# Half of the softmax transposes moved from TensorE to VectorE and DMA in a four-layer conditioned transformer

## The chip, the cores and the metric

The kernel runs on one core of a Trainium2 chip, in one launch. The metric is the device time in microseconds, the median of the runs shown. All data are 32-bit floats.

## The reference

Eight sequences of 256 tokens with 512 features pass through four layers, each steered by a conditioning vector per sequence.

- Layer 0: RMS norm, attention with 8 query heads of width 64 and one key and value head, rotary embedding; then a gated MLP of width 2048 (SiLU).
- Layer 1: layer norm with scale and shift, attention with 16 heads of width 32 on normalised queries and keys, an added bias, a gated residual; then an MLP of width 2048 (GELU).
- Layer 2: layer norm, attention with 16 query heads and 4 key and value heads of width 32, rotary embedding, and a block-sparse mask.
- Layer 3: eight small two-layer experts over slices of 64 features, a layer norm, SiLU and an output product.

What the change touches is the middle of each attention. For one head it is

```
s = q @ k.T (+ bias or mask)          # 256 x 256
p = exp(s - max(s))                   # rows are queries
y = (p @ v) / sum(p)
```

`p @ v` is summed over the keys. TensorE sums over the partitions, so p, which comes with queries on the partitions, has to be turned so that keys lie there.

## The kernel before, in words

**Scheduling.** The program is written against a layer that places tiles in buffers, sets the semaphores, and plans the order in which each engine's queue gets its instructions: it simulates the program and issues what is ready in the simulation, older instructions first. So an instruction can be issued ahead of an older one of the same engine. On the chip each queue then runs in that order. All DMAs of the kernel are issued from SP's queue (SyncE).

**Attention.** `attend` runs all three attentions. It works on groups of four heads: 2 groups per sequence in layer 0, 4 in layers 1 and 2, so 16, 32 and 32 groups. One iteration of its loop does, in the order of the source:

1. `scored`: the scores of the next group, for four heads and two query tiles, into four PSUM banks of tag `A` (line L645). Heads lie on separate groups of rows of the array and run side by side.
2. `turned` for heads 0 and 1 of the group before: each 128x128 block of p is transposed by TensorE with the identity (L702) into a bank of tag `C`, and `copy` brings it back over p, head 0 by VectorE (L460), head 1 by ScalarE (L464). A head has four blocks, and three in layer 2, where a tile of keys is hidden.
3. `softmax` of the next group: per head and query tile the row maximum (L659 in layer 0; L667, fused with the bias or mask, in layers 1 and 2) on VectorE, then the exponential with its row sum on ScalarE (L672). Then the reciprocals of the sums are turned, written to DRAM (`spread`, L685) and read back as a broadcast (L690).
4. `some`: a stretch of queued work. Generators hold the projections of the next sequence, the output product of the last one and sums of weights; each `some(quantum)` runs a share of it. `rest` runs all that is left, at the start of each sequence.
5. `turned` for heads 2 and 3 of the group before, then `some` again.
6. `weighted`: p @ v for the group before (L717), into one bank of tag `C`, and `divided`: the product with the broadcast reciprocals (L732, VectorE) into `ctxT`. A last `some`.

At the end of the layers 0 and 1 the last group's weighted sum is placed beside the start of the MLP (`then`, `mlp_begin`).

**Buffers.** p has 7 buffers of 128x512, one head each. `ctxT` has 6 of 128x256. `qk` has 4 of 128x512.

**Turning by blocks.** The normalised inputs of most sequences are already turned without TensorE: `prepare` writes them in an interleaved order, VectorE transposes every 32x32 block of the tile in one instruction (L515, 128x1024), four DMAs write it to DRAM (`turn`, L520), and `fetch` reads it back with the blocks in their places (L533 in one DMA, L539 in eight).

**MLP.** `mlp` of the layers 0 and 1 multiplies 2x2 blocks with seven products in place of eight (L908 up, L955 down). `blocked` and `blocked_again` hold the right-hand sums in three tiles of `ctxT` (for the first sequence in `qk`). L908 reads its moving operand from the turned tiles in runs of 32 elements. `sums` takes one p buffer per product. The tail of each MLP runs the next layer's first projection as queued work.

Of the kernel before, what the change touches and what calls it, by code (L numbers as in the profile page):

```python
# [25 lines left out]
F32 = mybir.dt.float32  # L27
# [6 lines left out]
P = 128  # L34
# [7 lines left out]
    "n": 4, "hT": 2, "qT": 2, "kT": 2, "v": 2, "ctxT": 6, "p": 7, "qk": 4, "row": 3, "wbig": 8,  # L42
# [48 lines left out]

def constants():
# [15 lines left out]
        "mask2": np.ascontiguousarray(mask),  # L108
    }


def layout(inputs):
# [10 lines left out]
    def grouped(w):  # L123
# [20 lines left out]
        "bias": np.ascontiguousarray(a["mask_1x1xSxS_ff0"].reshape(S, S)),  # L144
        "vec": np.ascontiguousarray(np.concatenate([vec[k] for k in VEC], 1)),
# [26 lines left out]
class Program:  # L172
# [50 lines left out]
    def setup(self):  # L223
# [40 lines left out]
        self.n_turn = 0  # L264
        self.half_pi = c([P, 1], "half_pi")
# [190 lines left out]
    def copy(self, i, out, in_, scale=None):  # L456

        if i % 2 == 0:
            if scale is None:
                self.nc.vector.tensor_copy(out, in_)  # L460
            else:
                self.nc.vector.tensor_scalar(out, in_, scale, None, ALU.mult)
        elif scale is None:
            self.nc.scalar.copy(out, in_)  # L464
        else:
            self.nc.scalar.activation(out, in_, AF.Copy, scale=scale)

    def modulated(self, i, out, in_, scale, shift):
        if shift is None:
            self.copy(i, out, in_, scale)  # L470
        elif i % 2 == 0:
            self.nc.vector.tensor_scalar(out, in_, scale, shift, ALU.mult, ALU.add)
        else:
            self.nc.scalar.activation(out, in_, AF.Identity, bias=shift, scale=scale)
# [27 lines left out]
    def prepare(self, name, b, quick=False):  # L502
# [14 lines left out]
        self.n_turn += 1  # L517
        to = kept.rearrange("(c i) (a x) -> a i c x", c=4, a=4)
        for a in range(4):
            nc.sync.dma_start(  # L520
                to[a], hT[32 * a : 32 * a + 32, :].rearrange("p (c x) -> p c x", c=4)
            )
        self.ready[name, b] = [hT, None, kept, 0]
# [17 lines left out]
    def h(self, name, b, quick=False):  # L541
# [16 lines left out]
        def placed(i, c, in_):  # L558
            scale = mod[:, scale_at + c, b : b + 1]
            shift = None if shift_at is None else mod[:, shift_at + c, b : b + 1]  # L560
            self.modulated(i, place[:, c], in_, scale, shift)

        if rows is None:
            for c in range(KC):
                placed(c, c, place[:, c])
# [43 lines left out]
    def attend(self, name, n_groups, hd, project, value, finish, work, key_tiles=(2, 2), biased=None,  # L609
# [27 lines left out]
        def scored(b, g):  # L637
# [3 lines left out]
            for j0 in range(0, 4, rows):  # L641
                for q in range(TB):
                    for j in range(j0, j0 + rows):
                        lhsT, rhs = lhs_rhs[j]
                        nc.tensor.matmul(  # L645
                            s[j][:, at[q] : at[q] + wide[q]], lhsT(q), rhs(wide[q]),
# [4 lines left out]
        def softmax(s):  # L651
            tot = self.t([P, 4, TB], "tot", 3)
            lows = self.t([P, 4, TB], "low", 3)
            ps = []
            for j in range(4):
                p = self.bank("p")[:, :total]
# [5 lines left out]
                for q in range(TB):  # L662
                    cols = slice(at[q], at[q] + wide[q])
                    src, sign = s[j], 1.0
                    if biased is not None:

                        nc.vector.tensor_tensor_reduce(  # L667
                            p[:, cols], s[j][:, cols], biased[:, cols], -1.0, BIG, ALU.add,
                            ALU.min, low[:, q : q + 1],
                        )  # L670
                        src, sign = p, -1.0
                    nc.scalar.activation(  # L672
                        p[:, cols], src[:, cols], AF.Exp, bias=low[:, q : q + 1], scale=sign,
                        accum_out=tot[:, j, q : q + 1],
                    )
                ps.append(p)
# [18 lines left out]
            return ps, by  # L695

        def turned(j, p):
# [9 lines left out]
            self.copy(j, p, m[:, :total])  # L707

        def weighted(b, g, pT):
            o = self.bank("C")  # L710
            for c in range(nch):
                for k in range(TB):
                    mine = [n for n, (kk, q) in enumerate(pairs) if kk == k]
                    q0 = pairs[mine[0]][1]
                    for i in range(per):
                        j = c * per + i
                        nc.tensor.matmul(  # L717
                            o[i * hd : (i + 1) * hd, c * S + q0 * P : (c + 1) * S],
                            value(got[b][1], g, j, k),
                            pT[j][:, mine[0] * P : (mine[-1] + 1) * P],  # L720
# [3 lines left out]
                        )  # L724
            return o

        def divided(b, o, by):
            for c in range(nch):
# [3 lines left out]
                nc.vector.tensor_tensor(out, in_, by[c], ALU.mult)  # L732
# [7 lines left out]
        for i in range(B * n_groups + 1):  # L740
# [17 lines left out]
            if last is not None:  # L758
                for j in range(2):
                    turned(j, last[2][0][j])  # L760
# [12 lines left out]
            elif ahead is None and then is not None:  # L773

                b, g, (pT, by) = last
                for j in range(2, 4):
                    turned(j, pT[j])
# [974 lines left out]
```

## Time and profile before

| what | value |
|---|---|
| time, median of 3 runs (lowest to highest) | 2129.92 us (2129.65 to 2131.94) |
| the profiled execution's own time | 2125.73 us |
| its span, from the first to the last instruction | 2123.8 us |
| mean granted TensorE clock | 0.994 of full speed |
| TensorE busy | 2060.5 us, 97% |
| VectorE, ScalarE, GpSimd busy | 1349.5, 761.1, 291.3 us |
| matmul instructions | 13282 |
| data moved by DMA | 138.18 MB |

The stages follow one another: the first loads, attention 0 to 304 us, the MLP of layer 0 to 895, attention 1 to 1296, the MLP of layer 1 to 1665, attention 2 to 1965, layer 3 to the end at 2124.

A row of a group reads: line, engine, operation, output tile and input tiles, shapes, count, then busy time in us, the mean of one in ns, and the idle time of the engine just before them with what ended it. Every 32-bit matmul stands in the profile as two instructions, a transpose as one. Matmuls overlap, so the mean of one is longer than the time from one start to the next. PE is TensorE, PEld its weight loads, DVE VectorE, ACT ScalarE, POOL GpSimd, SP SyncE, whose queue issues the DMAs. The chain is the work that ended last, followed back from the last instruction.

### The profile page before, as it was taken

To read this page: it belongs to the slowest core of one execution; us is meant where nothing else is said; L and a number is where in the kernel's file an instruction comes from. 1 tells how busy PE (TensorE), PEld (TensorE's weight loads), DVE (VectorE), ACT (ScalarE), POOL (GpSimd) and SP (SyncE) were. 2 spreads that over 40 slices of the span, in tenths; PEclk is the share of its full clock that TensorE was granted. 3 is DMA by queue.
4 is the path that set the end of the run, shared out by engine and by line. 5 is a ranking of instruction groups with operands and counts; after the bars stand their busy time and mean duration, and the time that the engine had idled before them with its cause. 6 is when DMAs were issued, how large, how long until landed. Compare 5 with 4: busy or idle time off the path is not lost.

```text
span 2123.8 us, 36492 instructions
## 1 busy us (share of the span) xinstructions
PE 2060.5 (97%) x13282; PEld 1523.8 (72%) x13282; DVE 1349.5 (64%) x4474; ACT 761.1 (36%) x2330; POOL 291.3 (14%) x308
## 2 busy tenths in 40 slices
PE   7999899999999999999999999999999989999999
PEld 4555569999999999855555547999999855555444
DVE  6856665656676555756666665776666777776333
ACT  3424321111111111245555663222222256566644
POOL 1101100000000000144444432000000101010220
PEclk9999999999999999999999999999999999999999
DMA  8320241211230100411112132233211222210001
GB/s 308 115 59 17 91 149 38 73 41 58 76 94 19 36 19 18 100 46 40 37 40 52 44 95 78 85 102 115 94 49 46 76 47 45 57 39 19 11 35 40
DMA packets 172147, 138.18 MB, mean 65 GB/s; under 512 B 77824, under 2 KB 144064, under 8 KB 171968
## 3 DMA queue, kind: packets, MB, share of 16 engines
q1 hardware_dynamic: 171968, 135.86, 21.6%
q8 instruction: 105, 1.72, 0.3%
q14 instruction: 74, 0.61, 0.1%
HBM read 99.87 MB, written 35.95 MB: 64 GB/s over the span
## 4 chain that ended last, share of the span: by engine, by line
PE 81%; DVE 8%; DMA 5%; ACT 2%; POOL 2%; issue 1%; SPq 1%; DVEq 0%; ACTq 0%; POOLq 0%
PE C L908 28%; PE C L585 20%; PE A L955 18%; PE C L702 4%; PE A L645 4%; PE C L717 3%; DMA wqkv<-spread 2%; DVE p L667 1%; PE A L1621 1%; DMA spread<-invT 1%; ACT p L672 1%; PE C L1639 1%; DMA turn<-hT 1%; DMA hT<-turn 1%; DVE p L460 1%
## 5 line engine op out<-in xcount | busy, mean ns | idle before, releaser
L908 PE MATMUL C<-hT,wbig 128*128 128x128 f32 x3072 | 416.3, 275 | 0.0
L908 PEld LDWEIGHTS C<-hT,wbig 128*128 128x128 f32 x3072 | 388.8, 192 | 8.6 <-issue 1.8
L585 PE MATMUL C<-wqkv,hT 128*128 128x512 f32 (+1 forms) x768 | 311.1, 545 | 4.9 <-DVE p L460 3.9
L908 PE MATMUL C<-ctxT,wbig 128*128 128x128 f32 x2160 | 300.0, 275 | 0.0
L672 ACT ACTIVATE p<-p,low 128x256 f32<-128x256 f32 (+1 forms) x512 | 241.9, 475 | 152.7 <-DVE low L667 152.0
L908 PEld LDWEIGHTS C<-ctxT,wbig 128*128 128x128 f32 x2160 | 270.1, 192 | 0.0
L955 PE MATMUL A<-wbig,p 128*128 128x256 f32 x1024 | 242.5, 379 | 0.0
L585 PEld LDWEIGHTS C<-wqkv,hT 128*128 128x128 f32 x768 | 130.9, 191 | 124.7 <-issue 111.2
L667 DVE CUSTOM_DVE_ANT_0 p<-A,row 128x256 f32<-128x256 f32 (+1 forms) x512 | 171.7, 386 | 70.6 <-PE C L717 55.1
L955 PEld LDWEIGHTS A<-wbig,p 128*128 128x128 f32 x1024 | 189.6, 190 | 23.0
L702 PEld LDWEIGHTS C<-ident,p 128*128 128x128 f32 x1152 | 129.3, 142 | 81.3 <-issue 39.6
L925 ACT COPY p<-C 128x128 f32<-128x128 f32 x192 | 51.3, 267 | 371.6 <-PE C L908 370.9
L936 DVE TENSOR_TENSOR p<-p,C 128x256 f32<-128x256 f32 x192 | 79.3, 421 | 162.7 <-PE C L908 160.8
L702 PE MATMUL C<-ident,p 128*128 128x128 f32 x1152 | 165.2, 282 | 15.2 <-DVE p L460 6.8
L585 PE MATMUL C<-wo,ctxT 128*128 128x512 f32 x336 | 158.7, 604 | 5.6 <-DVE ctxT L732 5.5
L439 POOL TENSOR_SCALAR r<-mv 128x2 f32<-128x2 f32 (+1 forms) x28 | 7.2, 256 | 953.0 <-DVE mv L432 953.0
L1276 ACT ACTIVATE p<-C 128x128 f32<-128x128 f32 x64 | 17.8, 278 | 295.9 <-DVE p L936 295.9
L926 DVE TENSOR_TENSOR p<-p,C 128x128 f32<-128x128 f32 x192 | 54.9, 286 | 101.5 <-ACT p L925 99.4
L460 DVE COPY p<-C 128x512 f32<-128x512 f32 (+1 forms) x160 | 100.7, 630 | 23.8 <-PE C L702 23.4
L585 PEld LDWEIGHTS C<-wo,ctxT 128*128 128x128 f32 x336 | 58.7, 190 | 70.5 <-issue 53.8
L672 ACT ACTIVATE p<-A,low 128x256 f32<-128x256 f32 x128 | 59.3, 478 | 120.5 <-DVE low L659 87.9
L464 ACT COPY p<-C 128x512 f32<-128x512 f32 (+1 forms) x160 | 85.5, 535 | 36.0 <-PE C L702 36.0
(226 smaller groups left out, 3064.7 us busy)
## 6 DMA issues: line engine op xcount, KB each, us to landing
turn<-hT SPq DMA_DIRECT2D x120, 128.0 KB
hT<-turn SPq DMA_DIRECT2D x16, 512.0 KB
kept<-hT SPq DMA_DIRECT2D x16, 512.0 KB
hT<-kept SPq DMA_DIRECT2D x16, 512.0 KB
wbig<-spread SPq DMA_DIRECT2D x64, 128.0 KB
hT<-turn SPq DMA_DIRECT2D x112, 64.0 KB
wbig<-in_wada1T SPq DMA_DIRECT2D x6, 1024.0 KB
ctxT<-kept SPq DMA_DIRECT2D x48, 128.0 KB
```

The costliest lines, as they stand in the source:

```text
L460: self.nc.vector.tensor_copy(out, in_)
L464: self.nc.scalar.copy(out, in_)
L585: self.nc.tensor.matmul(out, lhsT(k), rhs(k), start=(k == 0), stop=(k == n - 1))
L645: nc.tensor.matmul(s[j][:, at[q] : at[q] + wide[q]], lhsT(q), rhs(wide[q]), start=True, stop=True,)
L667: nc.vector.tensor_tensor_reduce(p[:, cols], s[j][:, cols], biased[:, cols], -1.0, BIG, ALU.add, ALU.min, low[:, q : q + 1],)
L672: nc.scalar.activation(p[:, cols], src[:, cols], AF.Exp, bias=low[:, q : q + 1], scale=sign, accum_out=tot[:, j, q : q + 1],)
L702: nc.tensor.transpose(m[:, n * P : (n + 1) * P], p[:, at[q] + k * P : at[q] + (k + 1) * P], self.ident,)
L717: nc.tensor.matmul(o[i * hd : (i + 1) * hd, c * S + q0 * P : (c + 1) * S], value(got[b][1], g, j, k), pT[j][:, mine[0] * P : (mine[-1] + 1 ...
L908: nc.tensor.matmul(m[:, c : c + P], w[:, k * P : (k + 1) * P], b[:, k], start=(first and k == 0), stop=(k == steps - 1), skip_group_check= ...
L926: nc.vector.tensor_tensor(g[:, 0, :], g[:, 0, :], m[:, P : 2 * P], ALU.add)
L936: nc.vector.tensor_tensor(g[:, 1:3, :], g[:, 0, :].unsqueeze(1).to_broadcast([P, 2, P]), m[:, 2 * P : 4 * P].rearrange("p (i t) -> p i t", ...
L955: nc.tensor.matmul(acc[at][:, half * S : (half + 1) * S], left, right, start=(p == 0 and half == 0), stop=(p == 3), skip_group_check=True,)
```

## The change

For heads 0 and 1 of every group TensorE no longer turns p. Their exponentials are written into one tile `blocks` of 128x1024 (128x768 in layer 2), with the columns in four interleaved quarters. When the third head's instructions have been issued, VectorE turns all 32x32 blocks of the tile in one instruction; `put` writes it to DRAM in four DMAs, and a fifth reads it back over the same tile. `weighted` reads heads 0 and 1 from there in runs of 32 elements. To make keys come out right, the scores of heads 0 and 1 are computed with the keys in another order (the moving operand of L645 is read in runs of 32), and bias and mask get a second copy in that order. Heads 2 and 3 are turned by TensorE as before, one before and one after the first `some`, and both are copied by ScalarE.

p becomes 4 buffers of 128x1024, each for two heads; `ctxT` goes from 6 to 4, and `three` puts the MLP's sums into `ctxT` for odd sequences and into `qk` for even ones. The first quarter of the layer-1 down weights, in whose tile the second bias lies, is loaded at the end of MLP 0 (`layer1_begin`), the second mask at the end of MLP 1 (`layer2_begin`).

TensorE's instructions are taken out of the planner's hands: they are issued in the order of the source. Some instructions of VectorE and ScalarE (`placed`, which scales a fetched input, and `divided`) are pinned behind all that the source gave their engine before.

```diff
-    ... "ctxT": 6, "p": 7, "qk": 4, ...
+    ... "ctxT": 4, "p": 4, "qk": 4, ...
...
+        self.flips = [self.tc.dram_tile([P, 8 * P], F32, name=f"flip{i}") for i in range(4)]
+        self.n_flip = 0
...
+    def put(self, kept, tile):
+
         to = kept.rearrange("(c i) (a x) -> a i c x", c=4, a=4)
         for a in range(4):
-            nc.sync.dma_start(
-                to[a], hT[32 * a : 32 * a + 32, :].rearrange("p (c x) -> p c x", c=4)
+            self.nc.sync.dma_start(
+                to[a], tile[32 * a : 32 * a + 32, :].rearrange("p (c x) -> p c x", c=4)
             )
...
             for c in range(KC):
-                placed(c, c, place[:, c])
+                self.tc.keep_in_program_order(placed(c, c, place[:, c]))
...
+                        keys = rhs(wide[q])
+                        if j < 2:
+
+                            keys = keys.rearrange("p (k c i) -> p c k i", c=4, i=32)
                         nc.tensor.matmul(
-                            s[j][:, at[q] : at[q] + wide[q]], lhsT(q), rhs(wide[q]),
+                            s[j][:, at[q] : at[q] + wide[q]], lhsT(q), keys,
                             start=True, stop=True,
                         )
...
-            ps = []
+
+            blocks = self.t([P, 8 * P], "p")[:, : 2 * total]
+            put = blocks.rearrange("p (c h x) -> p h c x", c=4, h=2)
+            plain = self.t([P, 2, 512], "p")
+            ps = [plain[:, j, :total] for j in range(2)]
             for j in range(4):
-                p = self.bank("p")[:, :total]
...
-                    src, sign = s[j], 1.0
+                    src, sign, out = s[j][:, cols], 1.0, ps[j - 2][:, cols]
+                    if j < 2:
+                        out = put[:, j, :, at[q] // 4 : (at[q] + wide[q]) // 4]
+                        src = src.rearrange("p (c x) -> p c x", c=4)
...
                     nc.scalar.activation(
-                        p[:, cols], src[:, cols], AF.Exp, bias=low[:, q : q + 1], scale=sign,
+                        out, src, AF.Exp, bias=low[:, q : q + 1], scale=sign,
                         accum_out=tot[:, j, q : q + 1],
                     )
-                ps.append(p)
+                if j == 2:
+                    nc.vector.transpose(blocks, blocks)
+                    kept = self.flips[self.n_flip % 4][:, : 2 * total]
+                    self.n_flip += 1
+                    self.put(kept, blocks)
+                    nc.sync.dma_start(blocks, kept)
...
-        def turned(j, p):
+        def turned(p):
...
-            self.copy(j, p, m[:, :total])
+            nc.scalar.copy(p, m[:, :total])
...
+            came = blocks.rearrange("p (a h n j) -> p h n a j", a=4, h=2, j=32)
+
+            def weights(j, mine):
+                if j < 2:
+                    ns = [at[pairs[n][1]] // P + pairs[n][0] for n in mine]
+                    step = ns[1] - ns[0] if len(ns) > 1 else 1
+                    return came[:, j, ns[0] : ns[-1] + 1 : step]
+                return plain[j - 2][:, mine[0] * P : (mine[-1] + 1) * P]
...
-                            pT[j][:, mine[0] * P : (mine[-1] + 1) * P],
+                            weights(j, mine),
...
+                        if j < 2:
+                            self.tc.keep_in_program_order(mm)
...
-                nc.vector.tensor_tensor(out, in_, by[c], ALU.mult)
+                self.tc.keep_in_program_order(
+                    nc.vector.tensor_tensor(out, in_, by[c], ALU.mult)
+                )
...
-                for j in range(2):
-                    turned(j, last[2][0][j])
+                turned(last[2][0][1][0])
...
-                for j in range(2, 4):
-                    turned(j, pT[j])
+                turned(pT[1][1])
...
+    def three(self, b):
+
+        if b % 2 == 1:
+            return [self.t([P, S], "ctxT") for _ in range(3)]
+        two = [self.bank("qk") for _ in range(2)]
+        return [two[0][:, :S], two[0][:, S:], two[1][:, :S]]
...
+        def two():
+            t = self.t([P, 8, P], "p")
+            return t[:, 0:4, :], t[:, 4:8, :]
...
-        with ExitStack() as ctx:
+        with ExitStack() as ctx, tc.manual_schedule(engines={mybir.EngineType.PE}):
             Program(ctx, tc, d, out).run()
```

## The prediction

> **What bounds the kernel now.** I read the page first, then the stages, then the groups of instructions, then one iteration of an attention, instruction by instruction, and last the DMA queue.
>
> ```profile
> PE 2060.5 (97%) x13282; PEld 1523.8 (72%) x13282; DVE 1349.5 (64%) x4474; ACT 761.1 (36%) x2330; POOL 291.3 (14%) x308
> PE 81%; DVE 8%; DMA 5%; ACT 2%; POOL 2%; issue 1%; SPq 1%; DVEq 0%; ACTq 0%; POOLq 0%
> ```
>
> TensorE is busy for 97% of the span and carries 81% of the chain that ended last. Work taken from it is time, as long as nothing new makes it wait. The busy time of each engine by stage, for the three attentions (PE, PEld, DVE, ACT, POOL, then clock and DMA share):
>
> ```profile
> 45.00:304.00 259.00, 242.04 (x1388) 143.88 (x1387) 174.42 (x492) 90.38 (x299) 36.88 (x63) 0.99 0.27 81
> 895.00:1296.00 401.00, 388.50 (x2220) 208.87 (x2219) 251.67 (x859) 221.41 (x676) 172.05 (x125) 0.99 0.20 52
> 1665.00:1965.00 300.00, 285.19 (x1937) 170.61 (x1937) 218.90 (x944) 166.64 (x623) 32.00 (x42) 0.99 0.21 49
> ```
>
> TensorE idles 17, 12 and 15 us in them; VectorE is at 63 to 73%, the DMA engines at a fifth to a quarter. Both gated layers between them have TensorE at 100% and are not touched in their matmuls. The groups that the change meets, with shapes kept apart:
>
> ```profile
> L702 PE MATMUL C<-ident,p 128*128 128x128 f32 x1152 | 165.2, 282 | 15.2 <-DVE p L460 6.8 <-ACT p L672 2.9 <-ACT qT L466 2.8
> L460 DVE COPY p<-C 128x512 f32<-128x512 f32 x96 | 65.6, 684 | 21.0 <-PE C L702 20.9
> L460 DVE COPY p<-C 128x384 f32<-128x384 f32 x64 | 35.1, 549 | 2.7 <-PE C L702 2.5
> L515 DVE STREAM_TRANSPOSE hT<-hT 128x1024 f32<-128x1024 f32 x30 | 37.1, 1236 | 0.3
> L667 DVE CUSTOM_DVE_ANT_0 p<-A,row 128x256 f32<-128x256 f32 x384 | 148.1, 419 | 34.3 <-PE C L717 27.3 <-PE A L645 7.0
> L908 PE MATMUL C<-hT,wbig 128*128 128x128 f32 x3072 | 416.3, 275 | 0.0
> L585 PE MATMUL C<-wqkv,hT 128*128 128x128 f32 x128 | 17.0, 275 | 0.0
> ```
>
> One iteration of attention 1, and a piece of attention 2, in order of time (start, duration):
>
> ```profile
> 1136.38 1.15 PE L645 MATMUL A<-kT,qT 32*128 32x256 f32 x16
> 1137.46 1.09 PE L702 MATMUL C<-ident,p 128*128 128x128 f32 x8
> 1138.39 1.88 PE L585 MATMUL C<-wqkv,hT 128*128 128x512 f32 x4
> 1140.63 0.49 ACT L672 ACTIVATE p<-p,low 128x256 f32<-128x256 f32 x1
> 1145.16 1.07 PE L717 MATMUL C<-p,v 128*32 128x256 f32 x16
> ...
> 1898.74 1.70 PE L645 MATMUL A<-v,qT 32*128 32x128 f32 x16
> 1901.61 0.50 ACT L672 ACTIVATE p<-p,low 128x256 f32<-128x256 f32 x1
> 1903.98 1.10 PE L717 MATMUL C<-p,v 128*32 128x256 f32 x16
> 1907.63 0.88 PE L702 MATMUL C<-ident,p 128*128 128x128 f32 x6 [0.55 <-ACT qT L466]
> 1908.44 0.94 PE L645 MATMUL A<-kT,qT 32*128 32x128 f32 x16
> ```
>
> Scores (L645), eight transposes, projections (L585), eight more, and the weighted sum (L717) of the group scored one iteration before. The ACT rows are the fourth exponential, which ends head 1: 4.7 and 3.4 us after the scores began. Last, an existing round trip of 512 KB through DRAM, and the queue when one batch's input is fetched:
>
> ```profile
> 333.82 1.77 SPq L520 DMA_DIRECT2D turn<-hT  x4
> 337.55 0.34 SPq L533 DMA_DIRECT2D hT<-turn  x1
> 252.18 3.94 DMA hT<-turn
> 1885.29 5.26 SPq L539 DMA_DIRECT2D hT<-turn  x8
> ```
>
> **The change part by part.** The sum is made against the profiled execution, 2125.7 us (span 2123.8); the median shown, 2129.9, is 4.2 above it, and I add that at the end.
>
> *Transposes removed.* 16 + 32 + 32 groups lose half of 16, 16 and 12 transposes: 128 + 256 + 192 = 576. Their busy mean (282 ns) overlaps; start to start, eight take 1138.39 - 1137.46 = 0.93 us, 0.116 each. 576 x 0.116 = **-67 us** of TensorE's path.
>
> *Evacuations.* VectorE copied heads 0 and 2, ScalarE 1 and 3; now ScalarE copies the two that are left. ScalarE's count is unchanged, VectorE loses 100.7 us (two L460 rows).
>
> *Block transposes added.* 48 of 128x1024 at 1.236 us, 32 of 128x768 at 3/4 of that (0.93, an estimate from the row): 89 us. VectorE ends 12 us lighter and stays at two thirds, so 0 on the path; with that cover gone they would cost the 89. The Trainium skill ("VectorE: DVE Perf Modes", Rules for kernel authors) speaks against this: a 128x128 transpose belongs on TensorE, VectorE turns only 32x32 blocks. By that rule the sum would be about +22 (89 added, 67 saved). The rows decide the other way: the engine that rule spares is at 65%, the one it loads at 97%.
>
> *The way through DRAM.* Four writes and one read per group, 400 issues on SP (about 2.1 us of it a group), 1 MB moved (0.75 in attention 2), 75 MB in all over 960 us, 79 GB/s more; the DMA share goes from a fifth to somewhat under a half. The row pair gives 3.73 us from the first write's issue to the read's, the chain 3.94 us for the read to land: 7.7. The skill ("DMA: Bandwidth & Descriptors", Anatomy of one DMA) has a fixed 2 us per DMA, most of it the write's receipt, plus bytes over 436 GB/s: 3.6 for four staggered writes plus 3.2 for the read, 6.8. I use the trace's 7.7; the rule would put the blocks back 0.9 us earlier, worth nothing in attention 1 and some 0.5 us a group in attention 2.
>
> When are they needed? Attention 1: head 1 done at 4.7, VectorE free and block transpose 1.6, trip 7.7: back 14.0 us after the scores began. The period falls from 11.7 to 10.8; the weighted sum stands 8.8 - 0.9 = 7.9 us into the next iteration: needed at 18.7. Slack 4.6, cost 0. Attention 0 has periods of 16 us: 0. Attention 2: 3.4 + 1.3 + 7.2 (three quarters of the bytes) = 11.9 against 7.7 (8.4 less 0.7) + 4.5 = 12.2. Slack 0.3. There, once per batch, the new input's four writes and its eight fetches (5.26 us of SP, last row) come between: the groups beside it come 1.7 and 3.3 us late, up to 1.4 and 3.0 us of idle TensorE, 8 batches: 0 to 35. I take **+15**. Behind the waiting read on SP stand the sums' spread and the broadcasts that divide the result; a read that waits 2 us for its writes holds them as long. Against that p's four double buffers hold two whole groups, where seven single ones did not: the 27.3 us that L667 waits for L717 (head 3 finding no buffer until the last weighted sum) should go, and the sums come earlier by as much. 0 for both.
>
> *TensorE in the order of the source.* I compared the order in which the trace ran the matmuls with the order in which the code before issues them: nearly the same. The planner ran 54 us of matmuls ahead of something older that was not ready, 22 of it transposes ahead of a batch's first scores (row 1907.63: six transposes before the scores, while the copy of q and k runs). In order, that gap stays empty. A seam then costs 0.3 (attentions 0, 2) to 0.7 us (1) of the saving: **+10**. The rest mostly filled idle time of the start-up: bounds -5 (VectorE's queue, now with the pinned copies, no longer blocks on a DMA early) and +32; I take **+6**, near the seams.
>
> *The three ends.* At the end of each attention no next scores hide the trip: the weighted sum comes 8.5 to 13 us after the last scores in the trace, the blocks at 12 to 14. 1 to 3.5 us each: **+7**; bounds 0 and +12.
>
> *Gathered operands.* Keys and blocks are read in runs of 32 elements. L908 reads its moving operand so and L585 reads 128 columns in one run: both 275 ns. 0; above, the row-tiled scores themselves show no such case: 0 to +30.
>
> *Waits of transposes on VectorE's copies.* 6.8 us in the L702 row, half of it or more: **-5**.
>
> *Moved loads and buffers.* Second masks (256 and 192 KB), `wfc2T`'s first quarter earlier, `ctxT` 6 to 4 and `three` alternating with `qk`: the loads lie under stages with TensorE at 100%; a chunk of ctxT is freed by the third projection step, which the source puts before the next division: 0, with 0 to +5.
>
> Sum: -67 + 15 + 10 + 6 + 7 - 5 = -34: 2125.7 - 34 = 2092, plus 4.2: **2096 us**.
>
> **The rivals.** *The blocks come late in every group of attention 2* (slower). Two groups are in flight, so when the weighted sum waits, two periods last the trip L plus the 3.2 us from a weighted sum to the next-but-one scores. At L = 12.2 nothing is lost, at 13.6 the old 8.4 is back, at 17 the period is 10.1: +54 there. With -30 and -15 from the other attentions and +23 of seams, order and ends: +32, 2162 us. It decides from a trip of about 15 us. For it: slack of 0.3, and SP waits in order (puts, read, spread, broadcast with their landings fill most of 7.7 us). Against: the quiet trip leaves 3.1 us to that point.
>
> *The order of the source takes the saving back.* If all 54 us come back as idle: -67 + 54 + 15 - 5 = -3: 2127 us. For it: the planner's order kept TensorE at 97%. Against: most of what it hoisted ran in gaps.
>
> *Gathered reads are slower than the L908 row says, or the planner lays SP so that every read blocks the broadcasts:* +50, 2180 us. Nothing in the rows speaks for it.
>
> **How the numbers follow.** Forecast 0.62, source order 0.15, late blocks 0.18, last 0.05. Best case: all 67 saved, 10 of relief, 17 lost: 2070. The forecast's own range is 2070 to 2118. The range reaches to 2145, into the late blocks; what lies beyond on either side is less than 0.2. About 0.2% (4.3 us) is what a measurement of this kernel can tell from no change. Faster: 0.62 + 0.4 x 0.15 = 0.68; same 0.07; slower 0.25.
>
> **What would show it.** Right: L702 at 576; periods near 10.8 and 7.8 us; L667 no longer waiting for L717; small PE waits on the blocks' DMA in attention 2 and at the ends. Wrong: L717 waiting for that DMA by a microsecond or more in most groups, a granted clock under 0.97 in attention 2, L645 or L717 with longer means, or idle PE ahead of a batch's first scores of over 2 us.

## The result, and the profile after

The changed kernel takes 2223.38 us (median of 4 runs, 2222.32 to 2227.35), the kernel before beside it 2129.78 us: a ratio of 1.0443, 95% interval 1.0425 to 1.0461. It is 94 us slower; 34 us faster had been forecast. The profiled execution spans 2221.3 us, at a mean granted TensorE clock of 0.965 (before: 0.994). From the page of the changed kernel, the same two lines as of before:

```profile
PE 2033.2 (92%) x12706; PEld 1475.8 (66%) x12706; DVE 1351.9 (61%) x4394; ACT 744.6 (34%) x2330; POOL 291.6 (13%) x308
PE 74%; DVE 8%; ACT 8%; DMA 5%; issue 3%; SPq 2%; POOL 1%; ACTq 0%; DVEq 0%; POOLq 0%
```

TensorE has 576 instructions fewer, yet its busy time fell by 27 us only, and ScalarE, which was hardly on the chain of work that ended last, now has 8% of it. The same three attentions, by stage (PE, PEld, DVE, ACT, POOL, then clock and DMA share); of these windows the first is that of before, the other two follow the shifted stages:

```profile
45.00:304.00 259.00, 226.50 (x1265) 131.64 (x1264) 172.62 (x466) 86.25 (x302) 37.95 (x63) 0.96 0.45 135
925.00:1310.00 385.00, 336.14 (x1791) 161.84 (x1789) 231.60 (x770) 200.60 (x641) 149.96 (x111) 0.96 0.47 126
1744.00:2054.00 310.00, 245.57 (x1548) 129.12 (x1550) 191.97 (x830) 150.94 (x592) 27.43 (x36) 0.88 0.44 112
```

In attention 2 TensorE idles 64 us of 310, and the clock is 0.88. VectorE is at 60 to 67% (63 to 73% before); neither it nor the DMA engines (under a half) is full. The groups that answer to those of before:

```profile
L730 PE MATMUL C<-ident,p 128*128 128x128 f32 x576 | 92.9, 288 | 0.0
L755 PE MATMUL C<-p,v 128*32 128x256 f32 x640 | 62.0, 411 | 33.8 <-DMA p<-flip 19.6 <-ACT p L735 13.3 <-ACT p L695 0.4
L660 PE MATMUL A<-kT,qT 32*128 32x256 f32 x640 | 50.5, 411 | 6.8 <-DVE kT L470 6.4
L596 PE MATMUL C<-wqkv,hT 128*128 128x512 f32 x640 | 314.9, 629 | 28.0 <-ACT hT L481 26.9 <-ACT v L1435 1.1
L691 DVE CUSTOM_DVE_ANT_0 p<-A,wbig 128x256 f32<-128x256 f32 x192 | 73.3, 419 | 30.8 <-PE A L660 30.8
L700 DVE STREAM_TRANSPOSE p<-p 128x1024 f32<-128x1024 f32 x48 | 59.7, 1243 | 9.8 <-ACT p L695 9.8
L700 DVE STREAM_TRANSPOSE p<-p 128x768 f32<-128x768 f32 x32 | 31.3, 978 | 1.7 <-ACT p L695 1.7
```

The transposes left are 576, and they wait for nothing. The scores with gathered keys (L660) have a mean of 411 ns where L645 had 404, the weighted sums 411 where L717 had 387, the stretches at half clock included. At full clock the sixteen matmuls of a group take what they took before, 1.15 us for the scores and 1.07 us for the weighted sum, so gathering is no cost that shows. The block transposes take 1.243 and 0.978 us (1.236 and 0.93 predicted). The maximum no longer waits for the weighted sum. The new thing is in the waits of TensorE, largest first (in all, times, longest):

```profile
PE C L596 <- ACT hT L481: 31.3, 7, 4.9
PE C L755 <- DMA p<-flip: 30.4, 10, 5.7
PE C L755 <- ACT p L735: 29.8, 28, 2.3
PE C L596 <- issue: 21.6, 5, 4.4
```

L596 is the projection, L481 the scaling of its input in `placed`, L735 the copy of a turned head. Before, no wait but that for the first load reached 7 us in all.

**Work, idle time, clock.** The clock record knows two states, full speed and half. So the span splits into three: TensorE idle; busy time counted at full speed; and the loss to the clock, half of the busy time that lies in half-speed stretches. I worked this out from the trace of every kernel below. The clock record begins 15 to 18 us into the span; what lies ahead of it counts as full speed.

| kernel | ratio to before (95%) | span | work at full speed | idle | lost to the clock |
|---|---|---|---|---|---|
| before | 1 | 2123.8 | 2047.6 | 63.3 | 12.9 |
| changed | 1.0443 (1.0425 to 1.0461) | 2221.3 | 1973.9 | 188.0 | 59.3 |
| b_order | 1.0208 (1.0192 to 1.0223) | 2166.5 | 2032.7 | 115.4 | 18.4 |
| a_planned | 1.0217 (1.0201 to 1.0232) | 2173.3 | 1992.1 | 120.3 | 60.9 |
| a_nopin | 1.0143 (1.0126 to 1.0160) | 2157.5 | 1972.2 | 146.6 | 38.6 |
| a_nodram | 1.0247 (1.0232 to 1.0262) | 2174.1 | 1974.9 | 156.6 | 42.6 |
| a_free | 1.0031 (1.0019 to 1.0044) | 2139.0 | 1976.2 | 116.4 | 46.4 |
| a_gq | 1.0066 (1.0048 to 1.0085) | 2146.7 | 1974.0 | 137.9 | 34.7 |
| a_split_nopin | 1.0079 (1.0064 to 1.0094) | 2145.7 | 1959.9 | 142.0 | 43.9 |
| a_fill | 1.0354 (1.0336 to 1.0371) | 2201.3 | 2012.5 | 158.0 | 30.8 |
| v_gq2 | 1.0013 (1.0004 to 1.0021) | 2126.3 | 1977.7 | 107.5 | 41.0 |
| v_ends | 0.9955 (0.9942 to 0.9969) | 2118.5 | 1980.8 | 100.7 | 36.9 |
| v_01 | 1.0061 (1.0048 to 1.0074) | 2141.4 | 2005.4 | 103.4 | 32.6 |
| v_last2 | 0.9976 (0.9967 to 0.9984) | 2119.7 | 1984.0 | 95.1 | 40.6 |

The work column is good to some 20 us: b_order has the matmuls of before and shows 15 us less, since the ends of matmuls are modelled. The saving is there: 74 us less work, 67 predicted. It is outweighed by 125 us more idle time and 46 us more loss to the clock.

**One seam.** A seam is the place where an attention takes up a new sequence. From attention 1 of the changed kernel, TensorE where the new sequence's projection begins, and ScalarE over the same time:

```profile
1076.81 1.15 PE L660 MATMUL A<-kT,qT 32*128 32x256 f32 x16 [0.95 <-DVE kT L470]
1077.89 1.09 PE L730 MATMUL C<-ident,p 128*128 128x128 f32 x8
1078.82 1.02 PE L596 MATMUL C<-wqkv,hT 128*128 128x512 f32 x2
1084.24 7.97 PE L596 MATMUL C<-wqkv,hT 128*128 128x512 f32 x14 [4.40 <-ACT hT L481]
1092.14 1.07 PE L755 MATMUL C<-p,v 128*32 128x256 f32 x16
...
1083.10 0.50 ACT L695 ACTIVATE p<-p,low 128x256 f32<-128x256 f32 x1
1083.50 0.19 ACT L695 ACTIVATION_READ_ACCUMULATOR p<-p,low 128x1 f32 x1
1083.60 1.08 ACT L481 ACTIVATE hT<-hT,mod 128x256 f32<-128x256 f32 x2
```

The scaling starts as the last of the group's eight exponentials ends. In the source it stands behind them, and the pin keeps it there. TensorE, also in the order of the source, may not go past the projection that waits for it, though the weighted sum of the group before (L755) follows in its queue. In attention 2 the same seam costs more (TensorE, then VectorE):

```profile
1867.29 0.87 PE L730 MATMUL C<-ident,p 128*128 128x128 f32 x6
1872.45 3.82 PE L596 MATMUL C<-hT,wqkv 128*128 128x256 f32 x8 [4.29 <-issue]
...
1871.08 0.98 DVE L700 STREAM_TRANSPOSE p<-p 128x768 f32<-128x768 f32 x1 [0.29 <-ACT p L695]
1871.98 0.69 DVE L480 TENSOR_SCALAR hT<-hT,mod 128x256 f32<-128x256 f32 x2
```

Here the wait is called "issue". It ends 0.1 us after the first of VectorE's two scalings (L480, 1871.98 to 1872.35). That one is pinned too, and it follows on the block transpose of the running group (L700), which the change added and which itself stands behind the exponentials of heads 0 and 1. ScalarE's scaling, which TensorE needs next, starts only at 1872.70, again behind its eight exponentials. Twelve seams wait in this way, six in attention 1 and six in attention 2: seven for ScalarE (the row of 31.3 us above) and five for VectorE (the row of 21.6), 53 us in all.

What follows the wait is slow as well. Before the change the eight matmuls took 1.73 us to the next start:

```profile
1807.77 1.89 PE L585 MATMUL C<-hT,wqkv 128*128 128x256 f32 x8
1809.50 1.88 PE L585 MATMUL C<-wqkv,hT 128*128 128x512 f32 x4
```

Here they take 3.62, since the clock record has half speed from 1870.0 to 1876.8. Away from seams and fetches the time from one group's scores to the next is near what was predicted: the last five of attention 2, where nothing is fetched, are 6.5, 7.2, 8.8, 6.5 and 8.4 us (7.8 predicted). At the seams it is 14 to 16 us there and 17 to 19 us in attention 1.

### The profile page after: what moved, and what is told of

Read it like the earlier page. It is cut to its first block, busy times and chain, and to the rows that moved or that the text cites. A ratio compares the mean times of both kernels' runs of the same rounds, so it can differ in the third digit from the quotient of the medians.

```text
span 2221.3 us, 36106 instructions
## 1 busy us (share of the span) xinstructions
PE 2033.2 (92%) x12706; PEld 1475.8 (66%) x12706; DVE 1351.9 (61%) x4394; ACT 744.6 (34%) x2330; POOL 291.6 (13%) x308
## 4 chain that ended last, share of the span: by engine, by line
PE 74%; DVE 8%; ACT 8%; DMA 5%; issue 3%; SPq 2%; POOL 1%; ACTq 0%; DVEq 0%; POOLq 0%
PE C L949 27%; PE C L596 19%; PE A L998 17%; ACT p L695 6%; PE C L755 3%; PE A L660 3%; DMA p<-flip 2%; DMA flip<-p 1%; PE C L730 1%; PE A L1680 1%; DVE p L691 1%; SPq L550 1%; ACT p L735 1%; PE C L1699 1%; DVE st L441 1%
## 5 line engine op out<-in xcount | busy, mean ns | idle before, releaser
L596 PE MATMUL C<-wqkv,hT 128*128 128x512 f32 (+1 forms) x768 | 328.7, 570 | 28.0 <-ACT hT L481 26.9
L596 PEld LDWEIGHTS C<-wqkv,hT 128*128 128x128 f32 x768 | 138.7, 202 | 159.7 <-issue 117.4
L596 PE MATMUL C<-wo,ctxT 128*128 128x512 f32 x336 | 160.9, 616 | 2.9 <-DVE ctxT L773 2.4
L949 PE MATMUL C<-qk,wbig 128*128 128x128 f32 x1152 | 160.9, 276 | 0.0
L949 PE MATMUL C<-ctxT,wbig 128*128 128x128 f32 x1152 | 160.0, 275 | 0.0
L949 PEld LDWEIGHTS C<-qk,wbig 128*128 128x128 f32 x1152 | 144.9, 193 | 0.0
L949 PEld LDWEIGHTS C<-ctxT,wbig 128*128 128x128 f32 x1152 | 144.1, 192 | 0.0
L755 PE MATMUL C<-p,v 128*32 128x256 f32 (+2 forms) x896 | 85.5, 398 | 42.8 <-DMA p<-flip 23.4
L691 DVE CUSTOM_DVE_ANT_0 p<-A,wbig 128x256 f32<-128x256 f32 (+1 forms) x256 | 84.5, 386 | 56.0 <-PE A L660 55.4
L1321 ACT ACTIVATE p<-C 128x128 f32<-128x128 f32 x64 | 17.7, 277 | 298.7 <-DVE p L979 298.7
L596 PEld LDWEIGHTS C<-wo,ctxT 128*128 128x128 f32 x336 | 61.1, 195 | 70.4 <-issue 58.4
L730 PEld LDWEIGHTS C<-ident,p 128*128 128x128 f32 x576 | 67.4, 145 | 56.8 <-issue 47.7
L755 PEld LDWEIGHTS C<-p,v 128*32 128x32 f32 (+1 forms) x896 | 34.4, 119 | 103.2 <-issue 38.6
```

What stands on the lines that cost most here:

```text
L596: self.nc.tensor.matmul(out, lhsT(k), rhs(k), start=(k == 0), stop=(k == n - 1))
L691: nc.vector.tensor_tensor_reduce(out, src, by, -1.0, BIG, ALU.add, ALU.min, low[:, q : q + 1])
L730: nc.tensor.transpose(m[:, n * P : (n + 1) * P], p[:, at[q] + k * P : at[q] + (k + 1) * P], self.ident,)
L755: mm = nc.tensor.matmul(o[i * hd : (i + 1) * hd, c * S + q0 * P : (c + 1) * S], value(got[b][1], g, j, k), weights(j, mine), start=(k == 0 ...
L949: nc.tensor.matmul(m[:, c : c + P], w[:, k * P : (k + 1) * P], b[:, k], start=(first and k == 0), stop=(k == steps - 1), skip_group_check= ...
```

## The experiments

All four theories speak of the same 94 us. A: the two orders, TensorE's and that of the pinned scalings, meet in a stall at each seam. B: the blocks come late from DRAM. C: the order of the source on TensorE alone. D: both copies on ScalarE. Gains below are differences of ratios times 2129.8. Spans of an attention run from its first to its last scores, in one profiled execution.

**a_nopin.** The scaling is free again; TensorE's order is exactly the changed kernel's.

```diff
-                self.tc.keep_in_program_order(placed(c, c, place[:, c]))
+                placed(c, c, place[:, c])
```

> The changed kernel, but the eight scalings of a sequence's turned input (hT by the modulation, on ScalarE and VectorE) are no longer held in program order on their engines; TensorE stays in the order of the source. Theory A (TensorE in the order of the source reaches a sequence's first projection while the scaling of its input stands pinned behind the running group's exponentials: 4.4 us of wait per sequence of attentions 1 and 2, 2.3 us of half-speed matmuls after it in attention 2): 16 stalls shrink to 1 us or less, 60 to 100 us faster than the changed kernel, 2125 to 2165 us. Theory B (the blocks' trip through DRAM is what costs): within 10 us of the changed kernel, about 2223.

Measured: 64 us under the changed kernel, in the range of A. Idle time falls by 41 us and the loss to the clock by 21. TensorE's waits for hT are gone, and the list now begins with

```profile
PE C L755 <- DMA p<-flip: 44.8, 17, 5.4
PE C L755 <- ACT p L735: 26.3, 26, 2.3
```

From its first to its last scores attention 1 takes 348 us (355 before, 385 changed), attention 2 still 282 (261 before, 310 changed). What is late next is the blocks' DMA: its wait grows from 30 to 45 us.

**a_planned.** The planner orders TensorE again, the pins stay.

```diff
-        with ExitStack() as ctx, tc.manual_schedule(engines={mybir.EngineType.PE}):
+        with ExitStack() as ctx:
```

> The changed kernel, but TensorE's order is again chosen by the planner; the pins on VectorE and ScalarE stay. Theory A: the planner can put the transposes and projections that are ready ahead of the late scaled input, so most of the 31 us wait for hT and of the half-speed matmuls behind it goes: 50 to 90 us faster than the changed kernel, 2135 to 2175. Theory C (the order of the source on TensorE alone is what costs, also at the start and the seams): faster still, 100 us or more, under 2125. Theory B: within 10 us of the changed kernel.

Measured: 48 us under the changed kernel, just short of A's 50 to 90. The wait for hT falls to 6.4 us, since other work goes ahead, and idle time to 120 us; but the loss to the clock stays at 61. Why so many short waits were left was not taken apart.

**b_order.** The kernel before, with TensorE in the order of the source and nothing else (the line above, the other way round).

> The kernel before, with one thing alone: TensorE in the order of the source. Nothing is pinned on VectorE or ScalarE and no blocks go through DRAM. Theory A: without the pins the order costs the seams and the start only, +10 to +30 us on the kernel before, 2140 to 2160. Theory C: +60 us or more, 2190 or above. Theory B: within 10 us of the kernel before.

Measured: 44 us slower than before, between the 10 to 30 of A and the 60 of C. Idle time grows by 52 us, spread over the three attentions (15 to 17 us each). Its largest waits:

```profile
PE C L585 <- DVE p L460: 18.5, 17, 1.8
PE C L483 <- DVE p L460: 9.6, 5, 6.4
PE C L483 <- DVE n L450: 9.3, 2, 5.7
```

No wait is large; many small ones that the planner had filled are open.

**a_nodram.** Only the blocks' way through DRAM is taken out; the weights of heads 0 and 1 are then not where they belong.

```diff
-                    self.put(kept, blocks)
-                    nc.sync.dma_start(blocks, kept)
```

> The changed kernel without the blocks' four writes and one read through DRAM: the 32x32 blocks are turned by VectorE but the weights of heads 0 and 1 are not brought to their places. Theory A: only the 30 us that the weighted sum waits for that DMA and some half-speed matmuls behind it go: 20 to 45 us faster than the changed kernel, 2178 to 2203. Theory B: the whole loss goes, 90 us or more, 2130 or under. If the crowded SP queue also delays the fetch of the next input, something between.

Measured: 42 us under the changed kernel, in the range of A. The trip is worth 42 us of the 94, with the waits for hT as they were (26.9 us for ScalarE's half, 24.9 for VectorE's). B is not the main cause, but far more than the 22 us that the prediction gave the trip, ends included.

**a_free.** Both orders to the planner (the two edits above together).

> The changed kernel with both orders given back to the planner: TensorE's, and that of the scaled input; the blocks and their way through DRAM stay. Apart these two gave 48 and 64 us. Theory A (the two orders meet at the same stall, so their gains overlap): 70 to 95 us under the changed kernel, 2125 to 2150. If they are separate costs the gains add: 2223 - 48 - 64 = 2111 or under, faster than the kernel before. Theory B (the blocks' DMA now sets attention 2): attention 2 stays over 280 us from its first to its last scores, and the kernel over 2140.

Measured: 88 us under the changed kernel, not 112: the two gains overlap by 24 us, as A said. The four kernels with and without the two orders make a table, in us over a_free:

| | scalings free | scalings pinned |
|---|---|---|
| TensorE by the planner | 0 (a_free) | 40 (a_planned) |
| TensorE in the order of the source | 24 (a_nopin) | 88 (changed) |

Each order costs something alone, and the two together cost 24 us more than their sum. The rest of the change with the planner is 6.6 us slower than the kernel before. `divided` stays pinned in all of these runs; what that costs was not tried. Attention 1 is 12 us shorter than before (343), attention 2 is 16 longer (277), and there the DMA is the first wait: 25.3 us, 14 times, of 49.7 in the whole kernel.

**a_gq.** On a_nopin, the eight fetches on another queue. SP's queue in attention 2 of the changed kernel shows why:

```profile
1885.12 0.78 SPq L532 DMA_DIRECT2D flip<-p  x2
1886.01 5.25 SPq L550 DMA_DIRECT2D hT<-turn  x8
1891.31 1.09 SPq L532 DMA_DIRECT2D flip<-p  x2
1892.49 0.56 SPq L713 DMA_DIRECT2D spread<-invT  x1
1893.50 0.30 SPq L532 DMA_DIRECT2D flip<-p  x1
1894.19 0.34 SPq L704 DMA_DIRECT2D p<-flip  x1
```

The scores of this group began at 1880.94. Its four writes are split by the eight fetches, and the read (L704) goes out 13.3 us after the scores, where it goes out after 7.6 us in groups without fetches. The weighted sum then waits 3.34 us.

```diff
-                    self.nc.sync.dma_start(to[:, k, t], parts[:, k, t])
+                    self.nc.gpsimd.dma_start(to[:, k, t], parts[:, k, t])
```

> The changed kernel with the scaled input free (as in a_nopin) and the eight DMAs that fetch a sequence's turned input issued on GpSimd's queue, not on SP's. Theory B' (the eight fetches, 5.3 us of SP, stand between a group's block writes and its read and delay them): the 45 us that the weighted sum waits for the blocks fall under 20, 20 to 40 us faster than a_nopin, 2120 to 2140. Rival (the DMA engines and not the issuing queue are what is crowded, or GpSimd issues them more slowly): within 8 us of a_nopin's 2158, or slower.

Measured: 16 us under a_nopin, twice the rival's limit and short of B'. The wait for the blocks falls to 21.8 us (between the first and last scores of attention 2 from 27.3 to 4.8) and attention 2 to 261 us, what it took before. Outside it, 10.5 us are lost once at the end of MLP 0. There the fetches of the next sequence stand behind GpSimd's own work and go out at 916.2 us, where SP issued them at 906.0 in a_nopin. VectorE waits for them with its scaling until 924.6, and behind the scaling stands a sum that GpSimd needs for attention 1's normalised queries and keys (L1428). The first waits:

```profile
PE C L755 <- ACT p L735: 29.1, 29, 2.3
PE C L755 <- DMA p<-flip: 21.8, 10, 5.2
PE C L1400 <- POOL qk L1428: 10.5, 1, 10.5
```

So the wait that went was for a place in SP's queue, not for the DMA engines, which move the same bytes.

**a_split_nopin.** On a_nopin, the copies of heads 2 and 3 shared between VectorE and ScalarE.

```diff
-            nc.scalar.copy(p, m[:, :total])
+            self.copy(j, p, m[:, :total])
```

> The changed kernel with the scaled input free (as in a_nopin) and the two copies of turned weights of a group shared again between VectorE (head 2) and ScalarE (head 3), not both on ScalarE. Theory D (both copies behind ScalarE's exponentials make the weighted sum wait 26 us): that wait falls under 12 us, 10 to 25 us faster than a_nopin. Rival (what the wait hides is the blocks' DMA, which comes at nearly the same time): that DMA's wait grows by as much, within 6 us of a_nopin's 2158.

Measured: 14 us under a_nopin, so D is a part. The wait for copies falls from 26 to 9 us (VectorE's and ScalarE's together); that for the blocks grows from 45 to 57, as the rival said, but by less than the 17 us gained.

**a_fill.** The changed kernel with 336 useless transposes (14 sequences of 24) ahead of the projections.

```diff
         if rows is None:
+            if not blocks:
+                m = self.bank("C")
+                for n in range(24):
+                    self.nc.tensor.transpose(m[:, n % 4 * P : (n % 4 + 1) * P], self.ident, self.ident)
```

> The changed kernel with work added: ahead of a sequence's first projection in attentions 1 and 2, 24 useless 128x128 transposes of the identity (0.116 us each at full rate, 2.8 us) that wait for nothing. Theory A with the clock (a wait of over 4 us is paid twice, since the matmuls behind it then run at half rate): the added work lies in the wait, the clock stays up, and the kernel gets faster by 10 to 30 us, 2190 to 2213. Rival (the half rate is only a side effect of the same lateness, and the projections' order sets the end): no gain, or up to 14 x 2.8 = 39 us slower, 2223 to 2262.

Measured: 19 us *faster* than the changed kernel, with 39 us of work added. The projection (L600 here) still waits for its input, but less:

```profile
PE C L600 <- ACT hT L481: 12.3, 11, 2.3
PE C L600 <- DVE hT L480: 8.2, 5, 1.8
```

Against these 39 us, idle time falls by 30 us and the loss to the clock by 28, from 59 to 31. The filler could at best take up the idle time it lies in, so what was gained beyond that is the clock: it is a cost of its own, not a mark of lateness.

**v_gq2.** On a_free, the queue of the fetches in attention 2 alone.

```diff
+            queue = self.nc.gpsimd if name == "attention2" else self.nc.sync
...
-                    self.nc.sync.dma_start(to[:, k, t], parts[:, k, t])
+                    queue.dma_start(to[:, k, t], parts[:, k, t])
```

> The changed kernel with both orders given back to the planner (as in a_free) and, in attention 2 alone, the eight fetches of a turned input on GpSimd's queue. If the crowded SP queue is what is left of attention 2's loss, attention 2 falls from 277 to 255 to 262 us between its first and last scores, and the kernel is 10 to 22 us under a_free, 2115 to 2127: faster than the kernel before by 0 to 14 us. Rival (with TensorE planned, the blocks' trip itself is too long for the shorter period): within 6 us of a_free.

Measured: 4 us under a_free by the ratios, as the rival said, and hardly clear of the noise. The profiled attention 2 falls by more, from 277 to 265 us, but a_free's profiled execution is the slowest of its six (2140.8 us) and v_gq2's the fastest of its thirteen (2128.1). Under the planner the queue matters less, and 43 us of waits for the blocks stay.

**v_ends.** On v_gq2, the last group of each attention turned by TensorE alone (its bias, keys and weights in plain order, four heads copied in turn).

```diff
+                flip = i < B * n_groups - 1
...
-                if j == 2:
+                if flip and j == 2:
```

> As v_gq2, but the last group of each attention has all four heads turned by TensorE and nothing sent through DRAM. In the changed kernel the last group of attention 1 waited 5.7 us for its blocks and lost 5 us to the clock behind it; in a_free the stage that holds this end is 12 us longer than before. If the ends are that trip: 15 to 25 us under v_gq2, 2095 to 2110. If they are something else (the copies on ScalarE, the planner): within 6 us of v_gq2.

Measured: 12 us under v_gq2, short of the 15 to 25 expected: 0.9955 of the kernel before (0.9942 to 0.9969), the fastest of all. The stage from the last scores of attention 0 to the first of attention 1 falls from 647 to 639 us, as expected; that after attention 1 by 3 us only, since the last group but one waits there in its stead:

```profile
PE C L765 <- DMA p<-flip: 9.7, 1, 9.7
```

**v_01.** Blocks in attentions 0 and 1 alone.

```diff
-                flip = i < B * n_groups - 1
+                flip = name != "attention2" and i < B * n_groups - 1
```

> As v_ends, but the blocks are used in attentions 0 and 1 alone; attention 2 turns all four heads on TensorE, as before the change. If attention 2's period (8.4 us) is too short for the trip, this is the better version: attention 2 back at 261 us, attentions 0 and 1 each 5 to 12 us shorter than before, 2108 to 2118. If v_ends gains in attention 2 too, it is under this one.

Measured: 1.0061 of the kernel before, and 22 us over v_ends. Attention 2 takes 289 us, though its transposes are those of before, which took 261. Its waits are small and for ScalarE's copies (11.7 us in 13 waits at the weighted sum, 11.1 at the transposes). Several differences from the kernel before are left: p's buffers come in pairs, `ctxT` has 4, `divided` is pinned, the fetches are on GpSimd's queue, and the copies of the heads go to the two engines in the other order. Which of them costs this was not tried. So the 22 us do not show what the blocks are worth in attention 2: with them it takes 270 us in v_ends, still longer than the 261 before.

**v_last2.** The last two groups.

```diff
-                flip = i < B * n_groups - 1
+                flip = i < B * n_groups - 2
```

> As v_ends, but the last two groups of each attention, not one, are turned by TensorE. In v_ends the last group but one of attention 1 still waited 9.7 us for its blocks, and the stage that holds this end kept 10.4 us of idle TensorE, where the kernel before has 0.9. If that is the trip with nothing left to hide it: that wait goes, 5 to 10 us under v_ends, 2110 to 2116. Rival (it moves to the next group back, or the added 24 transposes, 2.8 us, and their copies take it up): within 3 us of v_ends's 2120.

Measured: 0.9976, 4 us over v_ends: the rival, a little beyond its 3 us, and the two intervals just touch. The wait of 9.7 us does go, and idle time after attention 1 falls from 10.4 to 3.6 us; the longest wait left there, 5.0 us two groups earlier, was in v_ends too. The added transposes and copies leave 3 us of that gain, and the stage after attention 0, where no such wait was, loses 5.

## Why the prediction was wrong

The measured time lies 127 us over the forecast of 2096. Of these, 88 go when the two orders are freed (a_free, 2136.7). That is where the sum failed.

**Order of the source, +10 and +6, and the pins.** This is the step that failed. The prediction had found the 54 us that the planner ran ahead, and its second rival priced them in full at 2127 (without the 7 us of the ends). The forecast counted 16 of them, because "most of what it hoisted ran in gaps". The gaps were its value: b_order measures the order alone at +44. Worse, the pins were read as a relief ("no longer blocks on a DMA early", part of the bound of -5). They were never asked the question that the text asks of every other wait: what stands ahead of the scaling, and who waits for it? On ScalarE eight exponentials, some 5 us, stand ahead of it, and on VectorE the added block transpose; behind it, with its order fixed too, waits all of TensorE. Beside the rest of the change, the pins alone cost 40 us, the order alone 24, and both together 88: a chain across three engines.

**Transposes removed, -67.** Right: 74 us less work, to the some 20 us of that column.

**Block transposes, evacuations, gathered operands, p's buffers, 0.** Right for gathering and for p: L667's waits for L717 (27.3 us in the row shown) are gone. The block transposes took the time costed and lie under other work, but at the seams of attention 2, where the pinned scaling stands behind them. (VectorE as a whole ended 2 us heavier than before, not 12 lighter.) Wrong for the evacuations: ScalarE's count is unchanged, but a copy on ScalarE now stands behind exponentials each time, and 14 us came back when one of two went to VectorE. The transposes themselves no longer wait for copies, as the -5 said; the weighted sum does, 29.8 us.

**Late blocks in attention 2, +15, and the ends, +7.** Right in kind, too small. The quiet trip is as predicted: the read goes out 7.6 us after the scores and the periods come near 7.8. The disturbed trip was known too (the groups beside a fetch 1.7 and 3.3 us late). But the whole trip is worth 42 us. At the ends, the three stages after the last scores show 26 us more idle time and loss to the clock than before, not 7; without the trip (a_nodram) 7 of them are left. After attention 1 the weighted sum could start on the blocks 17.7 us after the last scores, not 14, and half speed lay over that end from 1317.0 to 1334.1 us.

**The clock.** The sum has no term for it; it is 46 of the 97 us that the span grew. The text named "a granted clock under 0.97 in attention 2" as a sign of failure, and it came (0.88), but its sum took each wait at its own length. Of the other signs, the weighted sum did not wait for the DMA in most groups (10 waits), and the idle time lay ahead of a sequence's projections, not of its first scores.

**The rivals.** No single one happened. The mechanisms of the first two did, each in part (42 us for the late blocks, 44 for the order), with the pins that none of them named. The third did not: gathered operands cost nothing that shows, and VectorE's division (L773) hardly waits for a DMA (9.2 us in all, 23.0 before).

## What to carry to other kernels

Where a change fixes the order of two engines, follow one item across both: find the instruction that the first engine may not pass, and then everything that the item's producer is held behind. Idle TensorE time that is dense enough to drop the clock costs more than its own length (here 46 us of clock beside 125 of idle time); so work taken away in a stretch that already waits saves little, and 39 us of work put there made this kernel faster. A transfer hidden in the steady state is bare at each end of a loop. There the old way can be kept, which gave 12 us and, with the two orders freed, the only kernels here that are faster than the one before (v_ends by 10 us, v_last2 by 5).

## What the runs showed of the hardware

**The clock goes by fixed windows, and they need not be idle.** All half-speed stretches in the records but the ones cut off by the end of the run are 1 to 6 times 3.41 us long, and those of one run start on one grid of that step. I divided the 14 profiles into windows of that grid, from where each clock record begins, and took the busy time of TensorE in each. At full speed, a window under 40% busy was followed by half speed every time (151 of 151); at 40 to 50%, 27 times of 53; at 50 to 70%, 27 of 292; from 70% on, 5 of 7846. At half speed, a window under 80% busy was never followed by full speed (0 of 135), one of 90% or more 202 times of 242. So 2 us without work in a window of 3.41 suffice, and thin work holds the clock down. The Trainium skill ("TensorE: Matmul & The Clock Gate", Part 1) has half speed after an idle window of about 3.4 us; the window agrees, the idleness it needs does not. How little the busy column shows of it, in two windows of 5 us of a_planned:

```profile
1750.00:1755.00 5.00, 1.19 (x16) 0.69 (x16) 4.83 (x11) 1.24 (x5) 1.49 (x1) 0.81 0.61 179
1755.00:1760.00 5.00, 5.00 (x31) 3.50 (x27) 3.92 (x14) 1.17 (x3) 1.38 (x3) 0.51 0.57 168
```

In the second, TensorE is busy for all 5 us at a clock of 0.51.

**An issuing queue can be the narrow place while the DMA engines are half idle.** With a DMA share of 0.47 in attention 2 of a_nopin, moving a sequence's eight fetches to another queue cut the wait for blocks there from 27.3 to 4.8 us (from 44.8 to 21.8 in the whole kernel) with the same bytes. What made the delay is seen in the order of issue: 5.25 us of fetches stand between the second and the third write of a group, and the read behind them.
